# A recurrent layer step by step on one core: one half's gate transposed in two operations of 32 columns

## The chip, the cores and the metric

The kernel runs on one core of a Trainium2 chip. The core's engines work side by side, each through its own queue of instructions in order: TensorE (PE; its weight loads are shown as PEld), VectorE (DVE), ScalarE (ACT), GpSimd (POOL) and SyncE (SP, which issues DMAs). They wait for each other by semaphores, and an instruction of VectorE that needs the written result of an earlier one of VectorE waits by a semaphore too. The metric is the device time of one execution in microseconds. Of 3 runs of the kernel before the median is 1639.87 us.

## The reference

A gated recurrent layer with a residual, float32, batch 8, 512 time steps, 512 units:

```python
def step(h, x_t):
    fused = jax.nn.sigmoid(jnp.concatenate([x_t, h], axis=-1) @ w_W + w_b)
    hidden_state, output_state = jnp.split(fused, 2, axis=-1)
    memory_state = x_t @ wx_W + wx_b + hidden_state * (h @ wh_W + wh_b)
    h_new = output_state * h + (1.0 - output_state) * jnp.tanh(memory_state)
    return (h_new, h_new)
_, hs = jax.lax.scan(step, h0, xT)
return x + jnp.swapaxes(hs, 0, 1)
```

In the kernel's names r is `hidden_state`, z is `output_state`, n is the tanh, and h the state. Each step needs the whole state of the step before.

## The kernel before

The 512 units are four quarters of 128. Quarters 0 and 1 are half A, 2 and 3 half B, and within a half the two quarters are the chunks c = 0 and 1. The state lies transposed for TensorE, units on the partitions: tile `hT[half][step]` is 128 x (2 chunks x 32 columns x 3 slots), where the 32 columns are 4 steps x 8 batch rows. Slot 2 is the state h, slot 0 a copy of it, slot 1 takes n.

**TensorE, one step.** The loop at L470 runs over the 512 steps. The order of the products is written out as `ORDER = "A0 A1 A2 A3 D0 D1 D2 D3 H2 H3"`: a letter is a PSUM bank and a digit a quarter of the state, which is the stationary operand (128x32); the moving one are weights. Each entry is four products, one for each group of 32 output rows. Bank A (256 columns) collects the h product of both halves and the z and r products of half A; bank D (128 columns) z and r of half B; bank H (64 columns) the remaining h product of half B. A0 and A1 need half A's new state and stream 256 columns, A2 and A3 need chunks 0 and 1 of half B's new state and stream 192. Behind them come three or four products of the x side, which don't need the state (bank xp). All record line L204. The profile shows each product as two passes, so A0 to A3 are 32 matmuls in a step, 4 of which run beside each other.

**VectorE and ScalarE, one step.** Results leave PSUM through transposes of VectorE in blocks of 32x32. In program order, the calls at L596 to L622 are:

- half A: transpose of r (`turn_r`, L521), of h (`turn_h`, L536), of z (`turn_z`, L521), then the marker memset of `settle` (L544); ScalarE takes the sigmoids (L244);
- `memory(0, 0)` and `memory(0, 1)`: for each chunk a scan on VectorE (L509, output m) that works out the tanh's argument, and the tanh on ScalarE (output hT, slot 1);
- transposes for half B: part of bank A (`turn_part`, L578), r from bank D (L521); ScalarE works out `sz`, the sigmoid of minus z for half B, 128x64, from bank D;
- `update(0, 0)`, the transpose of bank H (L536), `update(0, 1)`: an update is a scan over three slots that gives h + (1 - z)(n - h) for one chunk and writes the next step's `hT`;
- a marker (L544), then `memory(1, 0)`, `memory(1, 1)`;
- `turn_sz` (L570 to L575): the transpose of `sz` into `hd0B`, slot 2, both chunks in one operation of 64 columns, and a marker;
- `update(1, 0)`, `update(1, 1)`, then copies of the new state to slot 0 on ScalarE, and for some steps sums of the x side on VectorE (L404), a transpose of x (L283) and two memsets (L654).

A **marker** is a memset of one column of `idle` that is made to wait, by a dependency added by hand, for an earlier VectorE operation. Instructions of VectorE that stand behind it in the queue start only when that wait is over. `SYNC` is the kind of dependency that makes it a semaphore wait.

GpSimd adds the residual and makes sums for the x side; SyncE loads x and stores the output.

Of the kernel before, what the change touches and what calls it, by code (L numbers as in the profile page):

```python
# [24 lines left out]
SYNC = mybir.DependencyInfo(mybir.DependencyClass.Sync, mybir.DependencyReason.DATA)  # L25
# [29 lines left out]
def tile_cond_rnn_residual(  # L55
# [39 lines left out]
    nc = tc.nc  # L95
# [54 lines left out]
    def pair(n, name, rows, slots):  # L150

        return const.tile([P, 2, rows, slots], F32, name=name).rearrange("p c n s -> p n c s")
# [9 lines left out]
    hd0 = [[pair(n, f"hd0{n}{i}", m, 3) for i in range(2)] for n, m in (("A", B), ("B", 32))]  # L162
# [290 lines left out]
    for c in range(2, NCH):  # L453
# [3 lines left out]
        done = 0  # L457
        for w in range(TC):
            n = done
# [10 lines left out]
    for i in range(T):  # L470
        g, s = divmod(i, GS)
        c, t = divmod(i, TC)
# [85 lines left out]
        def turn_r_b():  # L558
            t_, _ = turned("r", 1)
            act(  # L560
                ("r", 1, g % 2, s),
                md0[1][g % 2][:, rows, :, 2].rearrange("p n c -> p c n"),
                t_,
                AF.Sigmoid,
            )
            sz = work.tile([P, HU], F32, tag="sz", name=f"sz_{i}")
            act(("sz", i % 4), sz, ps["D"][:, :HU], AF.Sigmoid, scale=-1.0)
            return sz

        def turn_sz(sz):  # L570
            inst = nc.vector.transpose(  # L571
                hd0[1][i % 2][:, :, :, 2].rearrange("p n c -> p c n"), sz
            ).ins
            mark = nc.vector.memset(idle[:, IDLE - 3 : IDLE - 2], 0.0).ins
            tc.add_manual_dep(mark, inst.name, SYNC)  # L575

        def turn_part():
            nc.vector.transpose(md1[1][g % 2][:, :, :, 0].rearrange("p n c -> p c n"), ps["A"][:, :HU])  # L578
# [24 lines left out]
        sz = turn_r_b()  # L603
# [8 lines left out]
        if i == T - 1:  # L612
# [5 lines left out]
            )  # L618
        memory(1, 1)
        turn_sz(sz)  # L620
        update(1, 0)
        update(1, 1)  # L622
# [136 lines left out]
```

## Time and profile before

| | |
|---|---|
| median of 3 runs | 1639.87 us (1639.54 to 1640.74) |
| the profiled execution | 1641.93 us, its span 1640.1 us |
| granted TensorE clock | 1.000 |
| busy: PE, PEld, DVE, ACT, POOL | 99%, 83%, 84%, 60%, 33% of the span |
| steps | 512, about 3.13 us each (A begins at 799.96, 803.09 and 806.23) |

How to read the rows. In the timeline a row has the start and the time covered in us, the engine, the line, the operation, output <- input, the shape, and how many instructions were merged into it; in brackets how long the engine sat idle before it and what ended that. In the table of waits a row has the engine, the tile and line that waited, what it waited for, the total in us, how often, and the longest. In the groups a row has the count, the busy time and the mean ns of one, then the idle time before them. Rows of a tile give the shortest, median and longest duration in ns.

### The profile page before, as it was taken

The page shows a single profiled execution, that of the slowest core. Times are in us where ns is not written, and L with a number is a line of the kernel's source. Part 1 is how long each engine was busy: PE and PEld are TensorE (multiplying, and loading weights), DVE is VectorE, ACT ScalarE, POOL GpSimd, SP SyncE. Part 2 cuts the span into 40 slices and gives each one's busy share as a digit, 9 for nine tenths or more (in the row PEclk, how much of TensorE's full clock was granted, in tenths as well). Part 3 has the DMA queues.
Part 4 walks back from the last instruction along what each step waited for, and adds up shares of the span by engine and source line. Part 5 has one row for each costly group of instructions (what it writes and reads, how often), then busy time and mean ns, then how long its engine had stood idle before and what let it go on. Part 6 is the DMA issues. An engine that isn't in the chain of part 4 may idle for free.

```text
span 1640.1 us, 125144 instructions
## 1 busy us (share of the span) xinstructions
PE 1626.5 (99%) x53006; PEld 1360.2 (83%) x53006; DVE 1385.0 (84%) x11239; ACT 976.9 (60%) x5520; POOL 548.9 (33%) x1443
## 2 busy tenths in 40 slices
PE   8999999999999999999999999999999999999998
PEld 5788888888888888888888888888888888888876
DVE  8888888888888888888888888888888888888886
ACT  3666666666555666656665656665666666666665
POOL 3333333333333333333333333333333333333220
PEclk9999999999999999999999999999999999999999
DMA  4000000000000000000000000000000000000000
GB/s 184 11 15 16 18 14 13 15 18 16 15 13 18 14 17 15 17 13 15 16 18 14 13 15 17 16 15 13 18 15 16 17 16 13 15 18 10 10 10 10
DMA packets 37291, 31.11 MB, mean 19 GB/s; under 512 B 4084, under 2 KB 35060, under 8 KB 36728
## 3 DMA queue, kind: packets, MB, share of 16 engines
q1 hardware_dynamic: 36576, 22.95, 4.5%
q8 instruction: 414, 6.78, 1.8%
q14 instruction: 149, 1.22, 0.3%
q10 hardware_dynamic: 152, 0.16, 0.0%
HBM read 14.70 MB, written 8.39 MB: 14 GB/s over the span
## 4 chain that ended last, share of the span: by engine, by line
PE 97%; DVE 1%; DMA 1%; issue 0%; SPq 0%; ACT 0%; DVEq 0%
PE A L204 48%; PE D L204 26%; PE xp L204 16%; PE H L204 7%; DMA wd<-in_wd_dram 1%; DVE tr L521 0%; DVE m L509 0%; DMA head<-in_xh_dram 0%; DVE md1B L578 0%; DVE md1A L536 0%; DVE tz L521 0%; DVE hT L509 0%; SPq L143 0%; ACT hT L244 0%; DVE idle L544 0%
## 5 line engine op out<-in xcount | busy, mean ns | idle before, releaser
L204 PE MATMUL A<-wa,hT 128*32 128x256 f32 x16352 | 884.1, 356 | 4.1 <-DVE hT L509 4.1
L204 PEld LDWEIGHTS A<-wa,hT 128*32 128x32 f32 x16352 | 507.9, 123 | 237.5 <-DVE hT L509 134.0
L204 PE MATMUL D<-wd,hT 128*32 128x128 f32 x16384 | 542.6, 273 | 1.0 <-DMA wd<-in_wd_dram 1.0
L204 PEld LDWEIGHTS D<-wd,hT 128*32 128x32 f32 x16384 | 482.3, 122 | 21.9 <-DMA wd<-in_wd_dram 1.3
L675 POOL TENSOR_TENSOR ot<-xin,hT 128x32 f32<-128x32 f32 x503 | 135.3, 269 | 1049.6 <-DVE hT L509 1038.1
L244 ACT ACTIVATE hT<-m 128x8 f32<-128x8 f32 x2048 | 324.1, 207 | 91.5 <-DVE m L509 91.3
L244 ACT ACTIVATE md0A<-tr 128x16 f32<-128x16 f32 x512 | 112.9, 220 | 409.5 <-DVE tr L521 409.5
L521 DVE STREAM_TRANSPOSE tr<-A 128x64 f32<-128x64 f32 x511 | 127.7, 250 | 221.0 <-PE A L204 220.8
L244 ACT ACTIVATE hT<-hT 128x16 f32<-128x16 f32 x1024 | 233.1, 228 | 85.0 <-DVE hT L509 84.1
L204 PE MATMUL H<-wa,hT 128*32 128x64 f32 x8208 | 210.0, 219 | 0.0
L204 PEld LDWEIGHTS H<-wa,hT 128*32 128x32 f32 x8208 | 187.3, 122 | 0.0
L509 DVE TENSOR_TENSOR_SCAN hT<-hd0B,hT 128x24 f32<-128x24 f32 x1024 | 154.5, 193 | 21.8
L509 DVE TENSOR_TENSOR_SCAN hT<-hd0A,hT 128x24 f32<-128x24 f32 x1024 | 171.9, 168 | 0.0
L509 DVE TENSOR_TENSOR_SCAN m<-md0B,md1B 128x24 f32<-128x24 f32 x1024 | 154.7, 193 | 0.0
L204 PE MATMUL xp<-ti,si 128*32 128x96 f32 x5040 | 150.1, 246 | 0.0
L509 DVE TENSOR_TENSOR_SCAN m<-md0A,md1A 128x16 f32<-128x16 f32 x1024 | 142.5, 181 | 4.8
L244 ACT ACTIVATE md0B<-tr 128x16 f32<-128x16 f32 x512 | 116.3, 227 | 42.8 <-DVE tr L521 1.3
L419 POOL TENSOR_TENSOR xs<-ff 128x192 f32<-128x192 f32 x240 | 140.6, 596 | 0.0
L578 DVE STREAM_TRANSPOSE md1B<-A 128x64 f32<-128x64 f32 x511 | 130.2, 255 | 0.0
L244 ACT ACTIVATE hd0A<-tz 128x16 f32<-128x16 f32 x512 | 116.6, 228 | 21.6
L536 DVE STREAM_TRANSPOSE md1B<-H 128x64 f32<-128x64 f32 x512 | 128.2, 250 | 0.1
L571 DVE STREAM_TRANSPOSE hd0B<-sz 128x64 f32<-128x64 f32 x512 | 126.4, 247 | 0.0
(103 smaller groups left out, 1916.4 us busy)
## 6 DMA issues: line engine op xcount, KB each, us to landing
out_dram<-ot SPq DMA_DIRECT2D x128, 64.0 KB, 1.6
xin<-in_x_dram SPq DMA_DIRECT2D x112, 64.0 KB, 2.5
wx<-in_wx_dram SPq DMA_DIRECT2D x4, 768.0 KB, 6.8
wa<-in_wa_dram SPq DMA_DIRECT2D x4, 512.0 KB, 9.6
wd<-in_wd_dram SPq DMA_DIRECT2D x1, 768.0 KB
xin<-in_x_dram SPq DMA_DIRECT2D x3, 256.0 KB, 9.2
wd<-in_wd_dram SPq DMA_DIRECT2D x1, 256.0 KB, 11.2
head<-in_xh_dram ACTq DMA_DIRECT2D x1, 144.0 KB, 4.8
```

The costliest lines, as they stand in the source:

```text
L204: nc.tensor.matmul(out_, lhsT, rhs, start=start, stop=False, skip_group_check=True)
L244: inst = nc.scalar.activation(out_, in_, func, **kw).ins
L419: nc.gpsimd.tensor_tensor(to, a, b, ALU.add)
L509: return nc.vector.tensor_tensor_scan(*[t_[:, :, c_].rearrange("p n c s -> p (n c s)") for t_ in (out_, d0, d1)], 0.0, ALU.mult, ALU.add,).ins
L521: inst = nc.vector.transpose(t_.rearrange("p c n -> p (c n)"), raw[n][hf]).ins
L536: inst = nc.vector.transpose(md1[hf][g % 2][:, :, :, hf].rearrange("p n c -> p c n"), raw["h"][hf]).ins
L571: inst = nc.vector.transpose(hd0[1][i % 2][:, :, :, 2].rearrange("p n c -> p c n"), sz).ins
L578: nc.vector.transpose(md1[1][g % 2][:, :, :, 0].rearrange("p n c -> p c n"), ps["A"][:, :HU])
L675: pool_done[i + 1] = nc.gpsimd.tensor_tensor(ot[:, t], x_of(c, slice(0, NQ), t, 1), hTs[(i + 1) % NH][:, :, :, B * s1 : B * s1 + B, 2].rea ...
```

## The change

Half B's `sz` (128x64) is transposed in two operations of 32 columns, chunk 0 first, in place of one of 64. The marker behind them waits for the first operation only. The order of the calls stays.

```diff
         def turn_sz(sz):
-            inst = nc.vector.transpose(
-                hd0[1][i % 2][:, :, :, 2].rearrange("p n c -> p c n"), sz
-            ).ins
+            done = [
+                nc.vector.transpose(hd0[1][i % 2][:, :, q, 2], sz[:, 32 * q : 32 * q + 32]).ins
+                for q in range(2)
+            ]
             mark = nc.vector.memset(idle[:, IDLE - 3 : IDLE - 2], 0.0).ins
-            tc.add_manual_dep(mark, inst.name, SYNC)
+            tc.add_manual_dep(mark, done[0].name, SYNC)
```

In the built program VectorE's queue for one step, from the transposes on, reads as follows. The order on the other engines is the same as before.

```
before                                        after
L571 transpose hd0B<-sz 128x64                L572 transpose hd0B<-sz 128x32 (chunk 0)
L574 memset idle, waits for L571              L572 transpose hd0B<-sz 128x32 (chunk 1)
L509 update chunk 0, waits for its tanh       L575 memset idle, waits for chunk 0's transpose
L509 update chunk 1, waits for its tanh       L509 update chunk 0, waits for its tanh
                                              a wait alone, for chunk 1's transpose
                                              L509 update chunk 1, waits for its tanh
```

## The prediction

> **What bounds the kernel now.** I read the page first (busy shares, then the chain that ended last), then the table of waits, then the groups of instructions by shape in the even part of the run, and last one step in the timeline.
>
> ```profile
> PE 1626.5 (99%) x53006; PEld 1360.2 (83%) x53006; DVE 1385.0 (84%) x11239; ACT 976.9 (60%) x5520; POOL 548.9 (33%) x1443
> PE 97%; DVE 1%; DMA 1%; issue 0%; SPq 0%; ACT 0%; DVEq 0%
> ```
>
> TensorE is busy nearly all the time and the chain stays on it. That does not yet say that it always works at its pace, since a matmul that waits for its weights is counted as busy. The waits and the shapes tell more:
>
> ```profile
> DVE tr L521 <- PE A L204: 220.8, 505, 1.1
> PEld A L204 <- DVE hT L509: 134.0, 481, 0.4
> PE A L204 <- DVE hT L509: 4.1, 17, 0.2
> ```
>
> ```profile
> L204 PE MATMUL A<-wa,hT 128*32 128x256 f32 x7632 | 502.5, 379 | 1.5 <-DVE hT L509 1.4
> L204 PE MATMUL A<-wa,hT 128*32 128x192 f32 x7622 | 411.5, 333 | 0.0
> ...
> L204 PE MATMUL A<-wa,hT x16352: 326/373/423, 19.8 to 1634.8; 128*32 128x256 f32 x100, 128*32 128x192 f32 x100
> ```
>
> Once in nearly every step the weight loads of bank A sit waiting for a VectorE scan that writes the state. The 192-column matmuls of A (A2 and A3, 16 records a step, four running beside each other) have a shortest time of 326 ns but a mean of 333. If the excess sits in the first four of the 16, each of those is (333 - 326) x 4 = 28 ns too long, and because the four run together the step loses 28 ns. One step shows that it sits there:
>
> ```profile
> 803.09 1.72 PE L204 MATMUL A<-wa,hT 128*32 128x256 f32 x32
> 803.18 0.20 DVE L509 TENSOR_TENSOR_SCAN m<-md0B,md1B 128x24 f32<-128x24 f32 x1
> 803.20 0.06 DVE L544 MEMSET idle<- 128x1 f32 x1
> 803.30 0.18 DVE L509 TENSOR_TENSOR_SCAN m<-md0B,md1B 128x24 f32<-128x24 f32 x1
> 803.40 0.24 DVE L571 STREAM_TRANSPOSE hd0B<-sz 128x64 f32<-128x64 f32 x1
> 803.69 0.20 DVE L509 TENSOR_TENSOR_SCAN hT<-hd0B,hT 128x24 f32<-128x24 f32 x1
> 803.71 0.06 DVE L574 MEMSET idle<- 128x1 f32 x1
> 803.81 0.18 DVE L509 TENSOR_TENSOR_SCAN hT<-hd0B,hT 128x24 f32<-128x24 f32 x1
> 803.94 0.51 PEld L204 LDWEIGHTS A<-wa,hT 128*32 128x32 f32 x16 [0.27 <-DVE hT L509]
> 804.63 1.05 PE L204 MATMUL D<-wd,hT 128*32 128x128 f32 x32
> ...
> 803.96 0.70 PE L204 MATMUL A<-wa,hT 128*32 128x192 f32 x12
> 804.15 0.67 PE L204 MATMUL A<-wa,hT 128*32 128x192 f32 x12
> ...
> 803.42 0.21 ACT L244 ACTIVATE hT<-m 128x8 f32<-128x8 f32 x1 [0.18 <-DVE m L509]
> ```
>
> (The rows with x12 come from two narrow windows and merge the matmuls that run in them, so their starts are those of A2's first and second group of four.) From the second group at 804.15 to the first of D at 804.63 are three groups in 0.48, so 0.16 each; from the first group at 803.96 to the second it is 0.19. The group that loses is A2's first, whose weights began to load at 803.94, 0.02 before its place. A2 is the first matmul of the step that takes half B's new state, and that state comes from the first update of half B, the scan at 803.69: it ends at 803.89 and the load starts 0.05 later.
>
> So a step is TensorE work throughout, with one hole of 28 ns, and the way to that hole is: transpose of z (803.40, 0.24), the marker memset that waits for it and stands before the update, the update at 803.69. The markers' recorded starts lie 0.02 behind the scan that follows them in the queue (803.71 against 803.69, 803.20 against 803.18), so a marker's row tells only when its wait was over. Transpose start to update is 0.29: 0.245 for the transpose and 0.045 until the update begins.
>
> **The change, part by part.** (1) The first transpose shrinks from 64 to 32 columns. The nearest row is the same operation with the same output stride of three and a source in SBUF:
>
> ```profile
> L571 DVE STREAM_TRANSPOSE hd0B<-sz x512: 237/247/274, 20.1 to 1636.8; 128x64 f32<-128x64 f32 x171
> ...
> L283 DVE STREAM_TRANSPOSE md1B<-xs x254: 183/215/224, 28.3 to 1621.7; 128x32 f32<-128x32 f32 x127
> ```
>
> 247 against 215 ns: the wait can end 0.032 sooner, 0.215 + 0.045 = 0.26 after the start in place of 0.29.
>
> (2) The next thing that the update waits for is the tanh of the same 32 columns. It starts at 803.42 and takes 0.215 (0.21 in the row), so it ends 0.235 after the transpose began. What a VectorE scan needs behind an ACT result is seen where a scan has nothing else to wait for, at the start of half A's memory:
>
> ```profile
> 805.06 0.21 DVE L536 STREAM_TRANSPOSE md1A<-A 128x64 f32<-128x64 f32 x1
> 805.17 0.22 ACT L244 ACTIVATE md0A<-tr 128x16 f32<-128x16 f32 x1 [0.80 <-DVE tr L521]
> 805.19 0.21 DVE L521 STREAM_TRANSPOSE tz<-A 128x64 f32<-128x64 f32 x1
> 805.35 0.06 DVE L544 MEMSET idle<- 128x1 f32 x1
> 805.42 0.28 DVE L509 TENSOR_TENSOR_SCAN m<-md0A,md1A 128x16 f32<-128x16 f32 x2
> ```
>
> 805.17 + 0.22 = 805.39, the scan at 805.42: 0.033. The tanh thus allows the update at 0.235 + 0.033 = 0.268. That is later than the transpose's 0.26, so tanh takes over as the last wait, and the update moves from 0.29 to 0.268: 0.022 us sooner.
>
> (3) A second transpose of 32 columns stands between the first and the marker, an added instruction in each of the 512 steps. VectorE takes them in order, so the update can't start before the second has been taken in. The start of the run has one such pair, same shape, same tile kind, back to back:
>
> ```profile
> 28.20 0.18 DVE L509 TENSOR_TENSOR_SCAN hT<-hd0B,hT 128x24 f32<-128x24 f32 x1
> 28.30 0.29 DVE L283 STREAM_TRANSPOSE md1B<-xs 128x32 f32<-128x32 f32 x2
> 28.50 0.52 DVE L297 TENSOR_TENSOR tw<-wx,tw 128x384 f32<-128x384 f32 x1
> ```
>
> Both end 0.29 after the first began and the instruction behind them starts at 0.20. One alone takes 0.20 to 0.215, so they overlap, and the place for the update is free at 0.20, before the 0.268. That a marker is released while a later transpose is still running is in the rows above: the marker at 805.35 waits for the transpose of 805.06, and the one of 805.19 runs until 805.40.
>
> The Trainium skill, VectorE: DVE Perf Modes, section "The DRAIN you can't avoid", speaks against this part: a next operation doesn't start until the pipe of the one before is empty, and its advice for chained operations is to minimize their count. The pair at 28.30 does not follow that in its strict form. By the rule the second transpose would end near 0.42 and the update come near 0.465, 0.175 later than now, some 89 us over 511 steps.
>
> (4) The marker now waits for the first transpose only, so the second update needs a wait of its own for the second transpose. It already waits for its tanh, and in the order of the built program the added wait is an instruction of its own in VectorE's queue, before the second update of all 512 steps. The kernel before has such waits ahead of scans in three places of its first five steps alone (the row with x3 below). Behind it in the queue are the second update, the drains of the x side, the transposes of x and the next step's first transpose. The price of such an instruction is seen in the fifth step, where one stands between the marker and the scan:
>
> ```profile
> 35.73 0.24 DVE L536 STREAM_TRANSPOSE md1B<-H 128x64 f32<-128x64 f32 x1
> 35.76 0.23 ACT L244 ACTIVATE md0B<-tr 128x16 f32<-128x16 f32 x1
> 36.05 0.06 DVE L544 MEMSET idle<- 128x1 f32 x1
> 36.09 0.31 DVE L509 TENSOR_TENSOR_SCAN m<-md0B,md1B 128x24 f32<-128x24 f32 x2
> ...
> L509 DVEq EVENT_SEMAPHORE  x3: 21/21/21, 19.0 to 36.0; - x3
> ```
>
> The scan follows the marker's row by 0.045 where it otherwise precedes it by 0.02: 0.065. The second update would then come at 0.29 (end of the second transpose) + 0.05 (the wait's end) + 0.065 = 0.405, and stands at 803.81 - 803.40 = 0.41 now: nothing. It has room besides. A3's first group has its place one group of 0.162 behind 804.15, at 804.31, and the hole tells how late a load may start: A2's started 0.015 before its place and lost 0.028, so 0.043 before it loses nothing. That is 804.27, or 804.25 once the step is 0.022 shorter. The second update ends at 803.99 and its load could start at 804.04. About 0.21 of delay is covered by A2's own matmuls; beyond that A3 pays one for one. VectorE's other new work is covered by its idle time before each step's first transpose (220.8 us in 505 waits, 0.44 a step).
>
> (5) Nothing moves on TensorE, ACT, POOL or the DMA queues; the order on them is the same.
>
> **The sum.** TensorE's timeline carries the rest: the chain from the end of A to the update of half B is started by TensorE's own results and does not change, so 0.022 saved at the hole is 0.022 off every step that has the hole. The rows of waits count 481 + 17 = 498 such steps. 498 x 0.022 = 11.0 us. The profiled execution took 1641.93 us (span 1640.1); it would become 1630.9. The median of the runs is 2.06 lower than that execution, 1639.87, and becomes 1628.9; I say 1629. The bounds of this case: at most the whole hole, 511 x 0.028 = 14.3 us (1625.6), at least 0.018 a step, since a start is read to 10 ns (1639.87 - 498 x 0.018 = 1630.9).
>
> **The rivals.**
> - The whole hole goes (1625.6). The update would have to end 6 ns sooner still. For it: scans that follow other work closely are shorter, 0.18 at 803.81 against 0.20 at 803.69. Against: the update will still be waiting when it starts, as now.
> - No change (1639.9). The short transpose is no quicker in this place, or the update starts by something else at its old time. Against: the 247 and 215 ns both stand behind scans, and 0.29 is the transpose's end plus 0.045 in the step shown.
> - Slower, by the second transpose: the update starts only when the second transpose has ended too. Then it comes at 0.29 + 0.045 = 0.335, 0.045 later than now; a later load lengthens the hole one for one, 511 x 0.045 = 23.0 us, 1662.9. It decides as soon as the pair holds the update past 0.29. Against: the marker at 805.35 and the start at 28.50. For: no row has an update right behind such a pair. The skill's rule of (3) is the strong form of this one.
> - Slower, by the separate wait: it delays the second update by more than 0.21, three times what the row at 36.09 shows; at 0.25 it would cost 0.04 x 511 = 20 us, less the 11 gained, 1649.
>
> **How the numbers follow.** About 0.2% (3.3 us) is what a measurement of this kernel can tell from no change. Chances: forecast 0.70, whole hole 0.09, no change 0.09, second transpose 0.08, separate wait 0.04. Faster 0.79, same 0.09, slower 0.12. The range goes from the whole hole, 1625.5, to a gain of a third of the forecast, 1636.
>
> **What would show it.** In the profile after: the transposes L572 with 32 columns, 1024 of them near 0.20; the update of half B 0.265 to 0.27 behind the first of a pair; the load of A2 near 803.92 on the scale of the step above, and the mean of the 192-column matmuls of A near 328 ns in place of 333; the second update near its old distance of 0.41. The forecast is wrong if that distance grows beyond 0.6, if the update stays at 0.29 or later, or if the 256-column matmuls or the load of A0 take up a wait of their own.

## The result and the profile after

Median of 7 runs: 1634.75 us (1634.03 to 1635.57) against 1640.21 us (1639.54 to 1640.74) for the kernel before on 7 runs. The ratio is 0.9967, with a 95% interval of 0.9955 to 0.9978. The change makes the kernel faster, by 5.5 us; the forecast was 1629 us, 11 less than before. The profiled execution took 1635.57 us with a span of 1633.7, against 1641.93 and 1640.1 before: 6.4 us of span.

The page of the kernel after has the same engine at the bound and the same chain:

```profile
PE 1619.8 (99%) x53006; PEld 1362.0 (83%) x53006; DVE 1414.2 (87%) x11751; ACT 976.5 (60%) x5520; POOL 550.8 (34%) x1443
PE 97%; DVE 1%; DMA 1%; issue 0%; SPq 0%; DVEq 0%
```

TensorE is busy 6.7 us less with the same 53006 matmuls, and VectorE is busy 29 us more for 512 more instructions. The groups by shape of the kernel after, between 100 and 1600 us, show where TensorE's time went:

```profile
L204 PE MATMUL A<-wa,hT 128*32 128x256 f32 x7664 | 504.3, 379 | 2.0 <-DVE hT L509 1.9
L204 PE MATMUL A<-wa,hT 128*32 128x192 f32 x7656 | 407.5, 329 | 0.0
```

The 256-column matmuls are as before, 379 ns. The 192-column ones went from 333 to 329 ns; the shortest is 326. Read as in the prediction, the hole in front of A2's second group was (333 - 326) x 4 = 28 ns a step and is now (329 - 326) x 4 = 12 ns. The change takes 16 ns from the hole, and not all of it. Record by record the two traces agree: A2's first four matmuls take 354 ns in the median before and 338 after.

One step of the timeline after, for the same stretch of the step as shown of before, and then two narrow windows of it that take merged rows apart:

```profile
799.95 0.20 DVE L509 TENSOR_TENSOR_SCAN m<-md0B,md1B 128x24 f32<-128x24 f32 x1
800.07 0.18 DVE L509 TENSOR_TENSOR_SCAN m<-md0B,md1B 128x24 f32<-128x24 f32 x1
800.17 0.29 DVE L572 STREAM_TRANSPOSE hd0B<-sz 128x32 f32<-128x32 f32 x2
800.44 0.06 DVE L575 MEMSET idle<- 128x1 f32 x1
800.44 0.33 DVE L509 TENSOR_TENSOR_SCAN hT<-hd0B,hT 128x24 f32<-128x24 f32 x2
800.70 0.51 PEld L204 LDWEIGHTS A<-wa,hT 128*32 128x32 f32 x16 [0.27 <-DVE hT L509]
801.40 1.05 PE L204 MATMUL D<-wd,hT 128*32 128x128 f32 x32
...
800.19 0.22 ACT L244 ACTIVATE hT<-m 128x8 f32<-128x8 f32 x1 [0.18 <-DVE m L509]
...
800.44 0.21 DVE L509 TENSOR_TENSOR_SCAN hT<-hd0B,hT 128x24 f32<-128x24 f32 x1
```

Both transposes are done 0.29 after the first began, and the update starts 0.27 after it, where it took 0.29 before. The tanh ends at 800.19 + 0.22 = 800.41 and the update follows by 0.03: tanh is now the last wait. The first transpose took 0.20, so with 0.043 behind it the marker's wait would have allowed the update at 0.243 already. The weights of A2 start to load at 800.70, 0.05 behind the update's end at 800.65. The durations by tile and by line:

```profile
L572 DVE STREAM_TRANSPOSE hd0B<-sz x1024: 175/194/223, 20.5 to 1630.4; 128x32 f32<-128x32 f32 x171
L509 DVE TENSOR_TENSOR_SCAN hT<-hd0B,hT x1024: 203/208/211, 20.7 to 1630.7; 128x24 f32<-128x24 f32 x171
...
L509 DVEq EVENT_SEMAPHORE  x515: 21/21/21, 19.4 to 1630.6; - x172
```

The updates of half B take 208 ns in place of a median of 193 (0.20 for the first and 0.18 for the second in the step shown of before). The separate wait is there 512 times more.

To see which steps gained, I took the time from one first transpose of a step (L521, tr<-A) to the next in both traces, for the steps from the 21st on, and the median for each of the 16 places that a step can have in a block of 16 time steps (30 or 31 steps a place). In 14 places the step got 13 to 19 ns shorter, 16 on average. In one place nothing changed (3.270 us both), and in one the step got longer (3.134 to 3.141 us). The 16 medians, each times its count, sum to 1542.8 us before and 1536.1 after: 6.7 us, which the span shows as 6.4.

### The profile page after: what moved, and what is told of

It is laid out like the page before. It is cut to its first block, busy times and chain, and to the rows that moved or that the text cites. A ratio compares the mean times of both kernels' runs of the same rounds, so it can differ in the third digit from the quotient of the medians.

```text
span 1633.7 us, 126168 instructions
## 1 busy us (share of the span) xinstructions
PE 1619.8 (99%) x53006; PEld 1362.0 (83%) x53006; DVE 1414.2 (87%) x11751; ACT 976.5 (60%) x5520; POOL 550.8 (34%) x1443
## 4 chain that ended last, share of the span: by engine, by line
PE 97%; DVE 1%; DMA 1%; issue 0%; SPq 0%; DVEq 0%
PE A L204 48%; PE D L204 26%; PE xp L204 16%; PE H L204 7%; DMA wd<-in_wd_dram 1%; DVE tr L521 0%; DVE m L509 0%; DMA head<-in_xh_dram 0%; DVE md1B L579 0%; DVE md1A L536 0%; DVE tz L521 0%; DVE hT L509 0%; SPq L143 0%; DVE idle L544 0%; DVE hd0B L572 0%
## 5 line engine op out<-in xcount | busy, mean ns | idle before, releaser
L521 DVE STREAM_TRANSPOSE tr<-A 128x64 f32<-128x64 f32 x511 | 127.8, 250 | 204.5 <-PE A L204 204.1
L509 DVE TENSOR_TENSOR_SCAN hT<-hd0B,hT 128x24 f32<-128x24 f32 x1024 | 172.0, 208 | 0.8 <-DVE hT L509 0.8
L572 DVE STREAM_TRANSPOSE hd0B<-sz 128x32 f32<-128x32 f32 x1024 | 149.3, 191 | 0.0
```

What stands on the lines that cost most here:

```text
L509: return nc.vector.tensor_tensor_scan(*[t_[:, :, c_].rearrange("p n c s -> p (n c s)") for t_ in (out_, d0, d1)], 0.0, ALU.mult, ALU.add,).ins
L521: inst = nc.vector.transpose(t_.rearrange("p c n -> p (c n)"), raw[n][hf]).ins
L572: nc.vector.transpose(hd0[1][i % 2][:, :, q, 2], sz[:, 32 * q : 32 * q + 32]).ins
```

## The experiments

Each ran beside the kernel before, whose median was between 1639.9 and 1641.3 us from one group of runs to the next, so the ratios are compared. The edits are against the changed kernel unless another is named.

**Is it the start of the first update that counts, one for one?** The split stays, the marker waits for both:

```diff
-            tc.add_manual_dep(mark, done[0].name, SYNC)
+            tc.add_manual_dep(mark, done[1].name, SYNC)
```

> Two transposes of 32 columns as in the changed kernel, but the marker waits for the second of them. It undoes the shorter wait and keeps the split. My theory (the time goes by when the first update of half B starts, one for one): the second transpose ends 0.29 us after the first began, the update starts 0.043 behind it, at 0.333 in place of 0.290 before and 0.267 in the changed kernel. The hole in front of A2's second group grows from 0.029 to about 0.075 in the steps that have it, about 450 x 0.046 = 21 us: 1661 us. Rival (the two transposes run one behind the other): update at 0.42 or later, 1700 us or more. Rival (the split alone brought the gain, through the shorter transposes): 1635 us.

Measured: 1660.56 us against 1639.90, ratio 1.0126 (1.0112 to 1.0140). Its timeline and the rows of its updates:

```profile
805.39 0.29 DVE L572 STREAM_TRANSPOSE hd0B<-sz 128x32 f32<-128x32 f32 x2
805.73 0.20 DVE L509 TENSOR_TENSOR_SCAN hT<-hd0B,hT 128x24 f32<-128x24 f32 x1
805.75 0.06 DVE L575 MEMSET idle<- 128x1 f32 x1
...
L509 DVE TENSOR_TENSOR_SCAN hT<-hd0B,hT x1024: 179/192/204, 20.9 to 1655.8; 128x24 f32<-128x24 f32 x171
```

The update comes 0.34 after the first transpose began, 0.045 behind the end of the pair, and the step is 0.044 longer: the first theory, in place and price. Only a part of this hole shows as a longer record: the 192-column matmuls have a mean of 335 ns, which by the reading above gives 36 ns, and in addition A2 starts 896 ns behind A0 in place of 863. Both together are 72 ns, 44 more than before. The split by itself is a loss of 20.7 us; the shorter wait turns it into the gain. The two transposes overlap, or the update would be at 0.42. The update takes 0.20 here, the marker's row behind it again, and the second one 0.18.

**Does the separate wait cost anything?** A second marker carries the wait for the second transpose (the transposes are returned by `turn_sz`, and `mark_sz` holds the two lines of the marker):

```diff
         memory(1, 1)
-        turn_sz(sz)
+        turned_sz = turn_sz(sz)
+        mark_sz(turned_sz[0])
         update(1, 0)
+        mark_sz(turned_sz[1])
         update(1, 1)
```

> The changed kernel with a second marker memset, waiting for the second transpose, before the second update; the separate wait instruction of VectorE is gone. My theory (the separate wait lies off the path): the same as the changed kernel within 1 us, 1634 to 1636 us, first update at 0.267. Rival (the separate wait is what ate part of the gain, by the longer scans, 208 ns in place of 203 and 182): scans back at 203 and 182, hole 0.005 smaller, 1632.5 us.

Measured: 1633.77 us, ratio 0.9964 (0.9951 to 0.9976), the same as the changed kernel. The 192-column matmuls have a mean of 329 ns here too. The updates:

```profile
L509 DVE TENSOR_TENSOR_SCAN hT<-hd0B,hT x1024: 200/206/210, 20.8 to 1629.1; 128x24 f32<-128x24 f32 x171
```

The first update takes 208 ns in the median here too, so its length does not come from the separate wait; the second takes 203, where it took 208 behind the separate wait. The wait lies off the path, as forecast.

**Is tanh the next limit, and does the second transpose make the update longer?** In two kernels the first operation goes in front of the second memory scan. `early_whole` is the kernel before with its one transpose moved; `early_split` moves the first of two and has a marker for each (the list behind `sz` names the chunks that are transposed).

```diff
         memory(1, 0)
+        whole_sz = turn_sz(sz)
...
         memory(1, 1)
-        turn_sz(sz)
+        mark_sz(whole_sz)
         update(1, 0)
         update(1, 1)
```

```diff
         memory(1, 0)
+        first_sz = turn_sz(sz, [0])
...
         memory(1, 1)
-        turn_sz(sz)
+        second_sz = turn_sz(sz, [1])
+        mark_sz(*first_sz)
         update(1, 0)
+        mark_sz(*second_sz)
         update(1, 1)
```

> The kernel before with the one transpose of 64 columns moved in front of the second memory scan of half B; the marker stays behind that scan. The transpose is over long before the tanh, so the first update waits for the tanh alone. If the tanh is the next limit, it starts 0.267 us behind the old place of the transpose, as in the changed kernel. Second memory scan 0.15 later, second update near 0.52, which by my bound of 0.21 us of cover costs nothing. If the first update lasts 203 ns again (the second transpose right before it made it 208): hole 0.008, about 1632.5 us. If it lasts 208 anyway: 1634.5 us. If the cover is less than I say: slower than the changed kernel, up to 1645 us.

> Two transposes of 32 columns, the first in front of the second memory scan of half B, the second behind it, with a marker for each and no separate wait. The first update waits for the tanh alone (0.267), with a second transpose still right before it. Second update near 0.48. By my theory like the one whole transpose moved early if the neighbour does not matter (1632 to 1635 us); if a transpose that runs right before the update makes it 5 ns longer, it is 2 us slower than that one.

Measured: `early_whole` 1636.98 us, ratio 0.9982 (0.9973 to 0.9991); `early_split` 1635.92 us, ratio 0.9977 (0.9968 to 0.9986). `early_whole` lies in the range that its expectation gave for a shorter cover, though the cover is not the cause, as the next rows show; `early_split` lies just above the values expected, and below `early_whole`, where 2 us above it was the price of a longer update. A step of `early_whole`, and its updates:

```profile
800.13 0.20 DVE L509 TENSOR_TENSOR_SCAN m<-md0B,md1B 128x24 f32<-128x24 f32 x1
800.25 0.24 DVE L571 STREAM_TRANSPOSE hd0B<-sz 128x64 f32<-128x64 f32 x1
800.39 0.17 DVE L509 TENSOR_TENSOR_SCAN m<-md0B,md1B 128x24 f32<-128x24 f32 x1
800.61 0.43 DVE L509 TENSOR_TENSOR_SCAN hT<-hd0B,hT 128x24 f32<-128x24 f32 x2
...
L509 DVE TENSOR_TENSOR_SCAN hT<-hd0B,hT x1024: 203/208/210, 20.4 to 1631.5; 128x24 f32<-128x24 f32 x171
```

The transpose is over at 800.49 and the update still starts at 800.61, 0.48 behind the first memory scan; in the changed kernel it is 0.49 (799.95 to 800.44), in the one before 0.51 (803.18 to 803.69). So tanh is the limit. And the update takes 208 ns without a second transpose near it: that rival falls. In every kernel where tanh released the first update it took 208, and 203 where the marker did (before and `split_both`).

Most steps of `early_whole` gained what they gain in the changed kernel. The loss sat in one place of the 16, the same that lost in the changed kernel: 3.134 us before, 3.141 in the changed kernel, 3.199 in `early_split`, 3.229 in `early_whole`. In that step VectorE's first memory scan of half A waits for a sum of GpSimd. The pairs of rows are that place's step number 266, first before, then the changed kernel, then `early_whole`:

```profile
864.65 0.59 POOL L419 TENSOR_TENSOR ff<-ff 128x192 f32<-128x192 f32 x1
865.12 0.19 DVE L509 TENSOR_TENSOR_SCAN m<-md0A,md1A 128x16 f32<-128x16 f32 x1
```

```profile
861.41 0.61 POOL L419 TENSOR_TENSOR ff<-ff 128x192 f32<-128x192 f32 x1
861.84 0.23 DVE L509 TENSOR_TENSOR_SCAN m<-md0A,md1A 128x16 f32<-128x16 f32 x1
```

```profile
861.56 0.60 POOL L419 TENSOR_TENSOR ff<-ff 128x192 f32<-128x192 f32 x1
861.90 0.31 DVE L509 TENSOR_TENSOR_SCAN m<-md0A,md1A 128x16 f32<-128x16 f32 x1
```

The scan takes 0.19 when GpSimd's sum ends 0.07 before it would; otherwise it ends 0.05 behind the sum (862.07 after 862.02, 862.21 after 862.16). GpSimd starts each step's work when the second update of half B is done, so a later second update (about 0.10 later in `early_whole` than in the changed kernel) or a shorter step moves that sum further into the next step. In this place the sum that collides starts 0.975 us behind the end of the second update in all three kernels, and from that end to the next step's first transpose are 0.896 us before, 0.871 in the changed kernel and 0.774 in `early_whole`.

**Is it GpSimd's sum?** In that step the second of the two sums needs the first one's result and starts late. Another order of the seven sums of a block leaves no dependent pair in one step:

```diff
-            for n in range(7):
-                at_step(w0 + w + n // 2, (result, e, n))
+            for n, m in enumerate((0, 2, 1, 3, 4, 5, 6)):
+                at_step(w0 + w + n // 2, (result, e, m))
```

It was put into `early_whole`, into `two_marks`, into the kernel before and into the changed kernel.

> The kernel with the whole transpose moved early, and GpSimd's seven result sums of each block in the order 0, 2, 1, 3, 4, 5, 6, so that no two that depend on each other share a step. My theory: in the one step of 16 where the second sum waits for the first, GpSimd's sum ends about 0.80 us into the next step, and VectorE's first memory scan of half A, two inputs in SBUF as GpSimd's sum has, ends 0.047 behind it, 0.11 us late. With the new order the sum ends about 0.68 there and the scan at its usual 0.73: 31 steps x 0.11 = 3.4 us, from 1637.0 to 1633.6 us. Rival (the late second update delays something else in that step): unchanged, 1637 us.

> The changed kernel with a second marker in place of the separate wait, and the same new order of GpSimd's sums. By my theory the scan in the one step of 16 ends 0.024 us sooner and the step gets its gain of 0.016 to 0.02 back: 31 x 0.024 = 0.7 us less, 1633 us. If GpSimd's sums have no part in it: 1633.8 us as without the new order.

> The kernel before with the new order of GpSimd's sums alone. There the sum ends 0.68 us into the step, and 0.68 + 0.047 lies just under the scan's usual end of 0.73, so the order should change nothing: within 0.5 us of the kernel before. Rival (GpSimd's pairs of dependent sums cost time in every kernel): 0.7 us or more faster.

Measured: `early_whole` with the new order 1634.74 us, ratio 0.9960 (0.9947 to 0.9972), from 0.9982; `two_marks` with it 1634.32 us, ratio 0.9955 (0.9943 to 0.9968); the kernel before with it 1641.20 us, ratio 0.9998 (0.9989 to 1.0007), no change. The same step of `early_whole` with the new order:

```profile
860.25 0.60 POOL L419 TENSOR_TENSOR xs<-ff 128x192 f32<-128x192 f32 x1
860.72 0.19 DVE L509 TENSOR_TENSOR_SCAN m<-md0A,md1A 128x16 f32<-128x16 f32 x1
```

The sum ends at 860.85 and the scan takes 0.19 again. The step went from 3.229 to 3.119 us; 31 x 0.11 = 3.4 us is the expected gain, and 0.0022 of the kernel's time, 3.6 us, is the measured one.

The Trainium skill, SBUF — State Buffer, section "Who interferes with whom", states the mechanism: GpSimd and VectorE share one pair of ports, and where VectorE's operation has two inputs in SBUF and GpSimd's reads SBUF, the second to issue blocks fully until the first finishes. Both operations here are of that kind, and the rows agree in that the scan does not end before the sum does. It ends 0.05 us behind it and not its whole 0.19, so a part of the scan must lie beside the sum; that it is the ports that hold it, no run here shows.

**How late may the second update be?** The second transpose goes behind the first update:

```diff
-        turn_sz(sz)
+        mark_sz(*turn_sz(sz, [0]))
         update(1, 0)
+        mark_sz(*turn_sz(sz, [1]))
         update(1, 1)
```

> Two transposes of 32 columns, each with its own marker, the second one behind the first update: transpose, marker, update, transpose, marker, update. It doubles as a test of how late the second update may be. By my bound its load may start 0.28 us later than in the changed kernel (the update at about 0.58 behind the first transpose's start, 0.395 now). The second transpose starts about 0.11 behind the first update, ends 0.20 later, the second update starts near 0.62: 0.04 over the bound, A3 loses 0.04 in some 480 steps, 17 to 20 us against the changed kernel, 1650 to 1655 us. Rival (a cover much longer than 0.21 us): no slower than the changed kernel. Rival (much less cover): 1670 us or more.

Measured: 1672.38 us against 1641.34, ratio 1.0188 (1.0174 to 1.0202): as slow as the second rival, though not for its reason. (The 0.28 us of that expectation does not fit its own figures, 0.58 less 0.395 is 0.185; what follows goes by the 0.58.) A step's updates, the groups and the same place's collision:

```profile
804.83 0.20 DVE L572 STREAM_TRANSPOSE hd0B<-sz 128x32 f32<-128x32 f32 x1
805.09 0.21 DVE L509 TENSOR_TENSOR_SCAN hT<-hd0B,hT 128x24 f32<-128x24 f32 x1
805.46 0.20 DVE L509 TENSOR_TENSOR_SCAN hT<-hd0B,hT 128x24 f32<-128x24 f32 x1
...
L204 PE MATMUL A<-wa,hT 128*32 128x256 f32 x7476 | 497.2, 383 | 0.0
L204 PE MATMUL A<-wa,hT 128*32 128x192 f32 x7480 | 416.3, 340 | 0.0
...
880.04 0.60 POOL L419 TENSOR_TENSOR ff<-ff 128x192 f32<-128x192 f32 x1
880.27 0.42 DVE L509 TENSOR_TENSOR_SCAN m<-md0A,md1A 128x16 f32<-128x16 f32 x1
```

The second update starts 0.63 behind the first transpose, where 0.62 was expected. In the steps without a collision A3's first four matmuls take 359 to 364 ns where the shortest is 326, and A2's are as in the changed kernel in the median: 0.033 to 0.038 is lost at A3, where 0.04 was expected, so the bound of 0.21 us of cover held to about 0.02 us. In these steps that is all, a step of about 3.155 us. (The means of the rows shown, 340 and 383 ns, take in the steps with a collision, where A0 and A2 wait too.) But the second update now pushes GpSimd's sums into the next step in six places of 16: five steps are about 0.12 longer than before and one 0.24. The sum is 31 x (9 x 0.022 + 5 x 0.117 + 0.236) = 31.6 us, measured 31.0. The part that the expectation left out is the same collision.

**One chip for the candidates.** The changed kernel again, with the new order of sums alone, and with the second marker as well:

> The changed kernel itself once more, on the same chip as the two below, so that they are compared on one chip. 0.9967 of the kernel before, as measured, about 5.5 us less.

> The changed kernel with the new order of GpSimd's sums and nothing else. If the collision of GpSimd's sum with the first memory scan takes 0.024 us in one step of 16 here: 31 x 0.024 = 0.7 us less than the changed kernel, and the step in question at 3.117 us in place of 3.141. If not: the same.

> The second marker in place of the separate wait, and the new order of GpSimd's sums, once more. If the separate wait costs nothing: the same as the changed kernel with the new order within 0.5 us, and 0.7 us below the changed kernel. If it costs: 1 us or more below the changed kernel with the new order.

Measured against 1640.75 us: 1634.70 us, ratio 0.9965 (0.9953 to 0.9978); 1634.65 us, 0.9965 (0.9951 to 0.9978); 1634.07 us, 0.9958 (0.9946 to 0.9971). In the trace the new order does what was expected of it in the changed kernel (the step 3.119 us in place of 3.141 and 3.138, the scan 0.19), but 0.7 us does not stand out of the medians: they differ by 0.05. The second marker with the new order had the lowest ratio both times, 0.9955 and 0.9958; its intervals overlap those of the changed kernel, so that it beats it is not shown.

## Why the prediction was right or wrong

**The mechanism was right.** The hole in front of A2, its size and its cause, the shorter first transpose, tanh as the next wait, the free place behind the pair of transposes, a marker released while a later transpose runs, the separate wait off the path: the trace after shows each, and `split_both`, `two_marks` and `early_whole` each tested one of them. The update moved from 0.290 to 0.267 where 0.268 was forecast. The first transpose took 0.200 and not 0.215, which changed nothing because tanh came later. The second update stands at 0.40 (0.405 forecast).

**The size was wrong, at two factors of the sum, 498 x 0.022 = 11.0 us, and at a term that the sum left at nothing.** Measured: about 16 ns in 14 of 16 places, nothing in one and a loss in one.

- The factor 0.022 was the shift of the update's start, and the sum took the update's length as unchanged. A first update that tanh releases takes 208 ns, one that the marker releases 203; the load of A2 follows the end. 0.023 less 0.005 is 0.018, and the hole shrank by 16 ns. This is the larger part of the miss, 498 x 0.006 = 3.0 us, and it is why even the 0.018 that the prediction took as the least a step could gain was too much. The prediction asked whether the update would be shorter behind close work, and not whether it would be longer behind another releaser. What in the engine makes the 5 ns is open: for the first update the runs show that it goes with the releaser, and not with the neighbour or the separate wait.
- The factor 498 was the sum of two rows of the table of waits, 481 + 17, and these rows count waits and not steps. The last 17 steps have no products of the x side left, so A0 waits there for half A's state, with its load and its matmul, and A2's load waits again behind it. One of these steps of before:

```profile
1602.00 0.62 PEld L204 LDWEIGHTS A<-wa,hT 128*32 128x32 f32 x16 [0.40 <-DVE hT L509]
1602.00 1.79 PE L204 MATMUL A<-wa,hT 128*32 128x256 f32 x32 [0.24 <-DVE hT L509]
1602.92 0.51 PEld L204 LDWEIGHTS A<-wa,hT 128*32 128x32 f32 x16 [0.30 <-DVE hT L509]
```

  Each counted once, 463 steps have such a wait, and in 457 the first four matmuls of A2 are more than 5 ns over 326 (28 ns in the median). The others are the first 14, a step in 16, and a few more. The step in 16 has a fourth product of the x side, which is 0.16 longer on TensorE, so that the state is there in time. The profile of before shows it in such a step:

```profile
875.07 0.21 PEld L204 LDWEIGHTS xp<-ti,xin 128*32 128x32 f32 x8
875.24 0.21 PEld L204 LDWEIGHTS xp<-ti,so 128*32 128x32 f32 x8
875.40 1.41 PEld L204 LDWEIGHTS A<-wa,hT 128*32 128x32 f32 x32
```

  The 32 loads of A stand in one row there, without the idle time that splits them in other steps. No shortening can be had in those 30 steps. 35 steps too many at 0.016 are 0.6 us.
- Step (5) and the sentence that the chain from the end of A to the update "does not change" left out GpSimd. The step is 16 ns shorter, and the second update ends 11 ns later in it, since it takes 208 ns in place of 182. Both let GpSimd's sum reach further into the next step, and in one place of 16 the first memory scan, two transposes and the updates behind it come 0.024 later. That place lost its gain and 7 ns more: 31 x (0.016 + 0.007) = 0.7 us.

Together: 463 x 0.016 = 7.4 us less 0.7 is 6.7, the same as the sum of the medians above. What A2's first four matmuls take beyond 326 ns, summed over all steps, went from 13.1 to 6.8 us, about what the span lost. The runs' medians show 5.5 here and 6.1 when the kernel ran again, with an interval of some 2 us to either side.

**The rivals.** "No change" and "the whole hole" are both excluded: 12 of 28 ns are left. "The second transpose holds the update" is excluded for this kernel, and `split_both` shows that its price was right, 0.044 a step where 0.045 was worked out (20.7 us; 23.0 for all steps, less those without a hole). "The separate wait" is excluded, and `late_second` shows its bound right at the matmuls to about 0.02 us, while the way that a late second update takes through GpSimd was in no rival. The strong form of the rule that the prediction took from the Trainium skill, VectorE: DVE Perf Modes, section "The DRAIN you can't avoid", that the next operation starts only when the pipe is empty, does not hold for this pair: in the changed kernel the second transpose starts 0.109 us behind the first, which takes 0.200, and both are done in 0.291. The same section adds that a next operation that is not held starts earlier. The prediction left that out, so the page speaks less against the change than the prediction says.

## What to carry to other kernels

When a wait is made shorter, the next one takes over, and the saving is to be read at the end of the waiting operation, in the steps that really have the hole: count holes by the stretched or late operation of the bound engine, step by step, and not by the rows of a table of waits, where one step can stand several times (498 rows here, 457 steps with a hole). Splitting an operation pays only through the wait that it shortens; the split alone cost 20.7 us here. Before calling an engine off the path, look at what its work will lie beside after the shift: one second update 0.1 later, covered on TensorE, cost 3.6 us through GpSimd and a scan at the start of the next step.

## What the runs showed of the hardware that was not expected

- A VectorE scan with two inputs in SBUF ended 0.05 us behind a GpSimd sum that was already running and outlasted it: 0.19 us alone, 0.23, 0.31 and 0.42 beside sums that ended later.
- Half B's update, a scan over 24 elements, takes 182 ns right behind another update, 203 where a marker's wait ended last, and 208 where tanh did. The second update of the changed kernel takes 208 as well, though it starts 0.044 us behind the end of the separate wait and 0.057 behind its tanh, so ScalarE is not all that goes with 208.
- A pair of 32-column transposes back to back is done in 0.29 us where one of 64 columns takes 0.245 and one of 32 alone 0.20: a split operation is 0.045 us longer, and its first half 0.045 us sooner.
